# The last attention's tail scores in eight array tiles, and its full products in column tiles

## The chip, the cores and the metric

One core of a Trainium2 chip runs the whole program. The time is the device time of one execution, in microseconds (us). The median of three runs of the kernel before is given, and one further execution was taken with the hardware profiler.

## What is computed

The input `x` holds 16 batches of 256 channels by 512 positions. Four layers follow one another, each added to its input: a masked self-attention with 8 heads, a causal convolution of four taps, a GRU over 128 steps, and a second masked self-attention with 16 heads of 16 channels. Only the last layer is touched by the change:

```python
Q, K, V = (proj(Wq), proj(Wk), proj(Wv))          # 16 heads of 16 channels, 512 positions
att = einsum('bhqd,bhkd->bhqk', Q, K) / sqrt(Dh) + b[0]
att = att * m + (1 - m) * NEG_INF                 # m: 0/1 mask of the keys
y = einsum('bhqk,bhkd->bhqd', softmax(att), V)
x = x + y
```

The masks are drawn with a chance of about one half. Where no batch has more than 320 keys that count, the program takes the way described here. All numbers are fp32.

## The kernel before

The convolution and the recurrence are done together, and at about 1690 us `attend_together` begins the last attention. For each batch it gathers the keys that count into a table of `ROOM` = 320 rows: POOL scatters the rows to a table in memory (`send`), SyncE brings the table back (`fetch_table`). The 320 keys are three chunks, two of 128 and a tail of 64 (`TAILK`).

The 16 heads of a batch are worked in four groups of four heads. A head takes 32 rows (`R3`) of a 128-row tile: 16 rows of its own channels in one half, and one extra row that carries the mask or the maximum. Even and odd heads of a pair of tiles share the projection, made by one product of 128 columns (`heads`, L1381).

A group (`group`) does this:

- *Maxima.* Scores of the queries against the keys, heads in four row tiles of 32 rows (L1415, in two parts), and for the tail in two row tiles of 64 rows against keys laid out on a diagonal (L1421; `diagonal` writes that layout into the last 128 columns of `K`). DVE takes the maxima out of PSUM (L1430, L1435).
- *Shift.* The maxima are transposed (L1448) and added into the extra row of `Q`.
- *Scores for the exponentials.* Keys on the partitions, queries along the columns. For chunks 0 and 1 there are four products, one per head, on row tiles of 32 rows (L1461), each into a PSUM bank of its own. For the tail there are two products on row tiles of 64 rows, each for two heads: partitions 0 to 63 of the result belong to the one head, 64 to 127 to the other. ACT takes the exponentials into `E`, two banks at a time (L1468).
- *Weighing.* Each head's exponentials are multiplied with its values into 32 of the 128 partitions of one bank, so in four column tiles of 32 columns (L1475). For the tail the values `V3` hold an even head on partitions 0 to 63 and an odd one on 64 to 127, and two column tiles of 64 columns do it (L1479). ACT copies the sum out (L1488).

`gather` transposes the batch (L1323, L1338) and makes the values (L1351), which ACT spreads into `V` (L1360, L1366); `finish` divides by the sums of the exponentials and adds the input, on POOL, SyncE and DVE.

PSUM is eight banks: three pairs (`pairs`, tiles `s`) for scores, one bank (`banks`, `sm`) for transposes, projections and values, one (`accs`, `av`) for the weighed sum. A pair is held from the first product into it until its last reader is done.

The order of the instructions is made by a planner (`Plan`) before the program is built. Each piece of work is a node with an engine, an assumed duration, a priority (`gn`, the number of the group, and an offset), its predecessors and the buffers it takes. Repeatedly the planner looks at all nodes that could start, and takes, among those within 0.12 us of the earliest, the one of best priority. For TensorE a node also has a mode, its tiling: a change of mode adds 0.2 us, and a node of the current mode has its priority bettered by 0.25. On the chip the engines run this fixed order, and wait on semaphores.

Of the kernel before, what the change touches and what calls it, by code (L numbers as in the profile page):

```python
# [16 lines left out]
P = 128  # L17
# [233 lines left out]
def tile_kernel(ctx: ExitStack, tc: tile.TileContext, x, cond, Wq0, Wo0, W_ih, W_hh, b_ih, b_hh,  # L251
# [999 lines left out]
    def attend_together():  # L1251
# [3 lines left out]
        with ExitStack() as es:  # L1255
# [8 lines left out]

            NK, G, TAILK = 3, H3 * R3 // P, ROOM - 2 * P
# [3 lines left out]
            V3 = [t[:, 2].rearrange("p (m q s) r -> p m q s r", m=2, q=2) for t in V]  # L1269
# [23 lines left out]
            for i in range(2):  # L1293
                nc.gpsimd.memset(V[i], 0.0)
                for q, e in ((0, DK3), (1, 0)):
                    nc.gpsimd.memset(V[i][:, 0:2, q::2, e : e + 1], 1.0)
                    for odd in range(2):
                        nc.gpsimd.memset(V3[i][64 * odd : 64 * odd + 64, :, q, odd::2, e : e + 1], 1.0)
                nc.gpsimd.memset(NM[i], 0.0)

            def gather(b, g0):
# [42 lines left out]
                for c0 in range(0, NK, 2):  # L1344
# [3 lines left out]
                    def values(some=some, sm=sm, c0=c0):  # L1348
                        for c in some:
                            for kc in range(KC):  # L1350
                                nc.tensor.matmul(SM[sm.i][:, (c - c0) * D : (c - c0 + 1) * D],  # L1351
                                                 lhsT=XK[xk.i][:, kc, c * P : c * P + P], rhs=wv3T[:, kc],
                                                 start=(kc == 0), stop=(kc == KC - 1))
                    m = plan.add("PE", 0.86 * len(some), g0 - 1.6 + 0.2 * c0, moved + v_done + [banks.take(sm)] + ([] if c0 else [vs.take(v)]), values)
                    for c in some:
                        def spread(c=c, sm=sm, c0=c0):
                            src = SM[sm.i][:, (c - c0) * D : (c - c0 + 1) * D]
                            if c < 2:
                                dst = V[v.i][:, c].rearrange("p (h q) r -> p h (q r)", q=2).rearrange("p h (m i) -> p h m i", i=DK3)
                                nc.scalar.copy(dst[:, :, 0::3], src.rearrange("p (h m i) -> p h m i", m=2, i=DK3))  # L1360
                                return
                            src = src.rearrange("p (m s q i) -> p m s q i", m=2, q=2, i=DK3)
                            for q in range(2):
                                for odd in range(2):
                                    r = slice(64 * odd, 64 * odd + 64)
                                    nc.scalar.copy(V3[v.i][r, :, q, odd::2, DK3 * q : DK3 * q + DK3], src[r, :, odd::2, q])  # L1366
                        m2 = plan.add("ACT", 0.4 if c < 2 else 1.0, g0 - 1.6, [m], spread)
# [4 lines left out]
            def heads(b, hp, g0, mk, xk, x3, moved, turned, made):  # L1372
# [3 lines left out]
                for w, x_, X_, deps, name, n, dur in ((wq3T, x3, X3, turned, "q", T, 1.72), (wk3T, xk, XK, moved + [made], "k", ROOM, 1.1)):  # L1376
                    sm = banks.new()

                    def product(w=w, x_=x_, X_=X_, n=n, sm=sm):
                        for kc in range(KC):  # L1380
                            nc.tensor.matmul(SM[sm.i][:, 0:n], lhsT=w[:, kc, hp * P : (hp + 1) * P], rhs=X_[x_.i][:, kc, 0:n],  # L1381
                                             start=(kc == 0), stop=(kc == KC - 1))
                    m = plan.add("PE", dur, gp - 2.6 + 0.1 * (name == "k"), deps + [banks.take(sm)] + [(qs if name == "q" else ks).take(x) for x in (qt if name == "q" else kt)], product)
# [19 lines left out]
            def group(g, b, gn, qt, kt, ready, v, v_done):  # L1403
# [50 lines left out]
                for kc in range(NK):  # L1454
                    e = es_.new()
                    st = [pairs.new() for _ in range(2 if kc < 2 else 1)]

                    def scores(kc=kc, st=st):
                        for j in range(J if kc < 2 else 2):
                            r = slice(R * j, R * j + R) if kc < 2 else slice(2 * R * j, 2 * R * j + 2 * R)  # L1460
                            nc.tensor.matmul(S[st[j // 2].i][:, j % 2, :], lhsT=K[kt.i][r, kc * P : kc * P + P] if kc < 2 else K[kt.i][r, ROOM:],  # L1461
                                             rhs=Q[qt.i][r, :], start=True, stop=True)
                    m = plan.add("PE", 0.88, gn + kc / NK, [shifted] + [pairs.take(x) for x in st], scores, mode=32 if kc < 2 else 64)
                    scored.append(m)
                    done = []
                    for jp in range(len(st)):
                        x = plan.add("ACT", 1.05, gn + kc / NK, [m] + (done or [es_.take(e)]),
                                     lambda jp=jp, st=st, e=e: nc.scalar.activation(E[e.i][:, 2 * jp : 2 * jp + 2], S[st[jp].i], AF.Exp))  # L1468
# [3 lines left out]
                    def weigh(kc=kc, e=e):  # L1472
                        if kc < 2:
                            for j in range(J):
                                nc.tensor.matmul(AV[acc.i][R * j : R * j + R, :], lhsT=V[v.i][:, kc, 8 * (g // 2) + 2 * j + q],  # L1475
                                                 rhs=E[e.i][:, j], start=(kc == 0), stop=False)
                            return
                        for jp in range(2):
                            nc.tensor.matmul(AV[acc.i][2 * R * jp : 2 * R * jp + 2 * R, :],  # L1479
                                             lhsT=V3[v.i][:, g // 2, q, 2 * jp : 2 * jp + 2].rearrange("p s r -> p (s r)"),  # L1480
                                             rhs=E[e.i][:, jp], start=False, stop=True)
                    last = plan.add("PE", 0.88, gn + kc / NK + 0.2, done + v_done + ([accs.take(acc)] if kc == 0 else [last]), weigh,
                                    mode="c32" if kc < 2 else "c64")
# [93 lines left out]
```

## Time and profile before

| what | us |
|---|---|
| median of 3 runs | 2614.56 |
| lowest, highest | 2605.72, 2616.25 |
| the profiled execution: its time | 2617.86 |
| the profiled execution: its span, first to last instruction | 2616.1 |
| TensorE busy, share of the span | 2448.6, 94% |
| VectorE (DVE) busy | 1780.2, 68% |
| ScalarE (ACT) busy | 1016.1, 39% |
| granted TensorE clock, mean | 0.977 |

A line of a group names the kernel's line, the engine and operation, the tiles written and read, the part of the array used (rows*columns), and the size streamed. An fp32 product appears as two records, so four products in four tiles are x8. Records of one tiling overlap, so a record's duration isn't its cost: the distance from one piece's start to the next one's is. In the chain of work, `smC` is the single bank, `sC` the pairs, `avC` the weighed sum.

### The profile page before, as it was taken

The numbers are of one execution on the slowest core, as the hardware profiler recorded it, in microseconds if no ns is written. First come the engines' busy times: TensorE is split into PE (matmuls) and PEld (weight loads), VectorE is DVE, ScalarE is ACT, GpSimd is POOL, SyncE is SP. The second block draws the span as 40 slices with busy tenths as digits, with TensorE's granted clock in tenths as the row PEclk, the third lists the DMA queues.
The fourth block names the chain that finished last, engine by engine and source line by source line (L and its number), as shares of the span: only waits on it lengthen the run. The fifth ranks groups of instructions, "written<-read, shape, count | busy, mean of one in ns | idle before, by whom it ended". The sixth has DMA issues, their size and how long they took to land.

```text
span 2616.1 us, 100684 instructions
## 1 busy us (share of the span) xinstructions
PE 2448.6 (94%) x45506; PEld 1635.2 (63%) x45506; DVE 1780.2 (68%) x3810; ACT 1016.1 (39%) x2459; POOL 385.3 (15%) x382
## 2 busy tenths in 40 slices
PE   5999889959999999999999999789999999999995
PEld 3545444437888888888888888644444444444442
DVE  1578778866888888888888655455666566665652
ACT  2444444422333333333333332234444544555452
POOL 2333231210000000000000000132223222231113
PEclk9999999979999999999999999989999999999997
DMA  5222221130000000000000000010011100110001
GB/s 178 69 65 68 62 63 35 35 137 3 5 4 4 5 4 4 4 5 4 4 4 5 5 4 4 5 49 28 28 32 36 41 29 28 33 39 26 19 19 36
DMA packets 54738, 80.22 MB, mean 31 GB/s; under 512 B 15824, under 2 KB 33434, under 8 KB 54292
## 3 DMA queue, kind: packets, MB, share of 16 engines
q1 hardware_dynamic: 45076, 56.66, 7.1%
q0 software_dynamic: 9216, 16.96, 2.2%
q8 instruction: 360, 5.90, 1.0%
q14 instruction: 86, 0.70, 0.1%
HBM read 45.05 MB, written 36.75 MB: 31 GB/s over the span
## 4 chain that ended last, share of the span: by engine, by line
PE 80%; issue 6%; DMA 4%; DVE 4%; POOL 3%; ACT 1%; SPq 0%; POOLq 0%; another core or an unknown queue 0%; DVEq 0%; ACTq 0%
PE pr L1084 10%; PE pz L1084 9%; PE pn L1084 9%; PE sC L1461 8%; PE sC L1415 7%; PE avC L1475 5%; PE pt L1075 4%; PE pr L1063 4%; PE pz L1063 4%; PE smC L1381 4%; PE sC L1421 3%; PE avC L1479 2%; PE smA L908 2%; DMA backA<-result,goto 2%; PE smC L1351 2%
## 5 line engine op out<-in xcount | busy, mean ns | idle before, releaser
L1430 DVE TENSOR_REDUCE nmC<-sC 128x4 f32<-128x1024 f32 x256 | 301.8, 1221 | 208.5 <-PE sC L1415 206.8
L1468 ACT ACTIVATE wih<-sC 128x1024 f32<-128x1024 f32 x320 | 313.6, 1022 | 236.6 <-PE sC L1461 218.6
L1084 PE MATMUL pr<-whh,hist 128*32 128x128 f32 x8192 | 281.6, 275 | 14.2 <-DVE hist L1120 10.2
L1084 PEld LDWEIGHTS pr<-whh,hist 128*32 128x32 f32 x8192 | 218.8, 110 | 118.5 <-DVE hist L1120 51.1
L1084 PE MATMUL pz<-whh,hist 128*32 128x128 f32 x8192 | 279.6, 273 | 2.2 <-issue 2.2
L1084 PE MATMUL pn<-whh,hist 128*32 128x128 f32 x8192 | 278.9, 273 | 0.0
L533 DVE SCALAR_TENSOR_TENSOR yw<-xT,condT,yw 128x512 f32<-128x512 f32 x360 | 269.5, 749 | 6.8
L1063 PE MATMUL pr<-wih,xw 128*32 128x128 f32 x4096 | 222.6, 274 | 22.2 <-DMA wv3nat<-in_L_cond_Wv_dram 19.1
L1084 PEld LDWEIGHTS pz<-whh,hist 128*32 128x32 f32 x8192 | 237.3, 110 | 3.3 <-issue 3.0
L1084 PEld LDWEIGHTS pn<-whh,hist 128*32 128x32 f32 x8192 | 237.1, 110 | 0.1
L1461 PE MATMUL sC<-qC,kC 32*128 32x512 f32 (+1 forms) x1280 | 231.7, 632 | 0.4 <-ACT wih L1468 0.3
L1063 PE MATMUL pz<-wih,xw 128*32 128x128 f32 x4096 | 224.1, 274 | 3.7 <-issue 3.4
L1115 ACT ACTIVATE nn<-pre 128x64 f32<-128x64 f32 x256 | 65.7, 257 | 384.3 <-DVE pre L1113 377.0
L1108 ACT ACTIVATE r<-pr 128x128 f32<-128x128 f32 x256 | 71.0, 277 | 319.2 <-PE pr L1084 318.9
L881 DVE TENSOR_REDUCE whh<-smA 128x2 f32<-128x640 f32 (+2 forms) x211 | 150.2, 752 | 65.1 <-PE smA L873 46.2
L1415 PE MATMUL sC<-kC,qC 32*128 32x256 f32 x2048 | 185.5, 401 | 0.0
L297 POOL DMA_INDIRECT table<-xT,togo x128 | 133.5, 1043 | 248.2 <-DMA table<-xT,togo 169.4
L1516 POOL TENSOR_TENSOR aC<-aC,pbC 128x512 f32<-128x512 f32 x64 | 81.2, 1270 | 590.9 <-ACT wih L1468 287.7
L1075 PE MATMUL pt<-xw,wih 128*32 128x256 f32 x2048 | 166.8, 382 | 0.0
L1288 POOL MEMSET pbC<- 128x512 f32 x4 | 2.3, 625 | 1101.2 <-DVE xT L1092 1101.2
L1109 DVE STREAM_TRANSPOSE rT<-r 128x128 f32<-128x128 f32 x256 | 79.7, 311 | 118.8 <-ACT r L1108 102.4
L1415 PEld LDWEIGHTS sC<-kC,qC 32*128 32x128 f32 x2048 | 128.7, 184 | 46.2 <-issue 16.5
(178 smaller groups left out, 3853.8 us busy)
## 6 DMA issues: line engine op xcount, KB each, us to landing
xA<-in_x_dram SPq DMA_DIRECT2D x16, 512.0 KB
pbC<-sums SPq DMA_DIRECT2D x256, 32.0 KB
out_dram<-oC SPq DMA_DIRECT2D x32, 256.0 KB
table<-zeros SPq DMA_DIRECT2D x16, 320.0 KB
xsA<-table SPq DMA_DIRECT2D x16, 256.0 KB
result<-ocA SPq DMA_DIRECT2D x16, 256.0 KB
xsC<-table SPq DMA_DIRECT2D x16, 256.0 KB
wih<-in_L_cond_W_ih_dram SPq DMA_DIRECT2D x4, 768.0 KB
```

What stands on the lines that cost most here:

```text
L297: nc.gpsimd.indirect_dma_start(tables[b], bass.IndirectOffsetOnAxis(togo[:, f, b : b + 1], 0), xT[:, f, b], None, bounds_check=ROOM - 1, o ...
L533: nc.vector.scalar_tensor_tensor(acc, xT[:, f, :, lo : lo + WIN], condT[:, f, k : k + 1], xT[:, f, :, t0 : t0 + WIN] if k == 0 else acc, A ...
L881: nc.vector.tensor_reduce(dst[:, lo : lo + len(some)], SM[0:n, some[0] : some[-1] + 1, 0:ROOM], AX.X, ALU.max, negate=True)
L1063: nc.tensor.matmul(sets[k % 2][0 if g == GATE_R else 2][32 * j : 32 * j + 32].rearrange("p (f i) -> p f i", i=32), lhsT=x2, rhs=gates(wih, ...
L1075: nc.tensor.matmul(ps[32 * j : 32 * j + 32], lhsT=wih[:, kc, 2 * T + fo * P + 32 * j : 2 * T + fo * P + 32 * j + 32], rhs=parts[p][:, kc]. ...
L1084: nc.tensor.matmul(ps[32 * j : 32 * j + 32].rearrange("p (f i) -> p f i", i=32), lhsT=slot[:, f], rhs=gates(whh, f, j)[:, g], start=False, ...
L1381: nc.tensor.matmul(SM[sm.i][:, 0:n], lhsT=w[:, kc, hp * P : (hp + 1) * P], rhs=X_[x_.i][:, kc, 0:n], start=(kc == 0), stop=(kc == KC - 1))
L1415: nc.tensor.matmul(S[st[j // 2].i][:, j % 2, u * 2 * P : (u + 1) * 2 * P], lhsT=Q[qt.i][R * j : R * j + R, c : c + P], rhs=K[kt.i][R * j : ...
L1430: nc.vector.tensor_reduce(dst[:, :, :, e_at + 1], S[st[jp].i].rearrange("p j (u k) -> p j u k", u=2), AX.X, ALU.max, negate=True)
L1461: nc.tensor.matmul(S[st[j // 2].i][:, j % 2, :], lhsT=K[kt.i][r, kc * P : kc * P + P] if kc < 2 else K[kt.i][r, ROOM:], rhs=Q[qt.i][r, :], ...
L1468: lambda jp=jp, st=st, e=e: nc.scalar.activation(E[e.i][:, 2 * jp : 2 * jp + 2], S[st[jp].i], AF.Exp))
L1475: nc.tensor.matmul(AV[acc.i][R * j : R * j + R, :], lhsT=V[v.i][:, kc, 8 * (g // 2) + 2 * j + q], rhs=E[e.i][:, j], start=(kc == 0), stop= ...
```

## The change

The tail's scores for the exponentials are made by eight products instead of two: four heads (row tiles of 32 rows) by two halves of the queries (column tiles of 64 columns). A bank then holds one head: its tail keys against queries 0 to 255 on partitions 0 to 63, and against queries 256 to 511 on partitions 64 to 127, in 256 columns. These take two pairs where one was taken. Two exponentials of 2 x 256 columns replace one of 2 x 512.

The tail's values are kept twice, `V` chunk 2 with zeros on partitions 64 to 127 and `V4` with zeros on 0 to 63. The tail is weighed by eight products in four column tiles of 32 columns: for each half of the queries, each head, 256 columns over all 128 partitions, with the zeros dropping the other half.

The projections and the values are made by a new function, `columns`, in four column tiles of 32 columns in place of one product of 128, and get the planner's mode of the weighing, "c32". The tail scores have a mode of their own, "8". The planner's durations for the tail scores, their exponentials and the spreading of the tail's values are changed.

```diff
-            V3 = [t[:, 2].rearrange("p (m q s) r -> p m q s r", m=2, q=2) for t in V]
+            V4 = [work.tile([P, H3, R3], F32, tag=f"v4{i}", name=f"v4C{i}") for i in range(2)]
+            HALF = T // 2
...
                 nc.gpsimd.memset(V[i], 0.0)
+                nc.gpsimd.memset(V4[i], 0.0)
                 for q, e in ((0, DK3), (1, 0)):
                     nc.gpsimd.memset(V[i][:, 0:2, q::2, e : e + 1], 1.0)
-                    for odd in range(2):
-                        nc.gpsimd.memset(V3[i][64 * odd : 64 * odd + 64, :, q, odd::2, e : e + 1], 1.0)
+                    nc.gpsimd.memset(V[i][0:64, 2, q::2, e : e + 1], 1.0)
+                    nc.gpsimd.memset(V4[i][64:P, q::2, e : e + 1], 1.0)
...
+            def columns(ps, left, right, kc):
+
+                for j in range(4):
+                    r = slice(R3 * j, R3 * j + R3)
+                    nc.tensor.matmul(ps[r], lhsT=left[:, r], rhs=right, start=(kc == 0), stop=(kc == KC - 1))
...
-                                nc.tensor.matmul(SM[sm.i][:, (c - c0) * D : (c - c0 + 1) * D],
-                                                 lhsT=XK[xk.i][:, kc, c * P : c * P + P], rhs=wv3T[:, kc],
-                                                 start=(kc == 0), stop=(kc == KC - 1))
-                    m = plan.add("PE", 0.86 * len(some), g0 - 1.6 + 0.2 * c0, moved + v_done + [banks.take(sm)] + ([] if c0 else [vs.take(v)]), values)
+                                columns(SM[sm.i][:, (c - c0) * D : (c - c0 + 1) * D], XK[xk.i][:, kc, c * P : c * P + P], wv3T[:, kc], kc)
+                    m = plan.add("PE", 0.86 * len(some), g0 - 1.6 + 0.2 * c0, moved + v_done + [banks.take(sm)] + ([] if c0 else [vs.take(v)]), values, mode="c32")
...
-                            for q in range(2):
-                                for odd in range(2):
-                                    r = slice(64 * odd, 64 * odd + 64)
-                                    nc.scalar.copy(V3[v.i][r, :, q, odd::2, DK3 * q : DK3 * q + DK3], src[r, :, odd::2, q])
-                        m2 = plan.add("ACT", 0.4 if c < 2 else 1.0, g0 - 1.6, [m], spread)
+                            for dst, r in ((V[v.i][:, c], slice(0, P)),) if c < 2 else ((V[v.i][:, 2], slice(0, 64)), (V4[v.i], slice(64, P))):
+                                dst = dst.rearrange("p (h q) r -> p h (q r)", q=2).rearrange("p h (m i) -> p h m i", i=DK3)
+                                nc.scalar.copy(dst[r, :, 0::3], src[r].rearrange("p (h m i) -> p h m i", m=2, i=DK3))
+                        m2 = plan.add("ACT", 0.4 if c < 2 else 0.7, g0 - 1.6, [m], spread)
...
-                            nc.tensor.matmul(SM[sm.i][:, 0:n], lhsT=w[:, kc, hp * P : (hp + 1) * P], rhs=X_[x_.i][:, kc, 0:n],
-                                             start=(kc == 0), stop=(kc == KC - 1))
-                    m = plan.add("PE", dur, gp - 2.6 + 0.1 * (name == "k"), deps + [banks.take(sm)] + [(qs if name == "q" else ks).take(x) for x in (qt if name == "q" else kt)], product)
+                            columns(SM[sm.i][:, 0:n], w[:, kc, hp * P : (hp + 1) * P], X_[x_.i][:, kc, 0:n], kc)
+                    m = plan.add("PE", dur, gp - 2.6 + 0.1 * (name == "k"), deps + [banks.take(sm)] + [(qs if name == "q" else ks).take(x) for x in (qt if name == "q" else kt)], product, mode="c32")
...
-                    st = [pairs.new() for _ in range(2 if kc < 2 else 1)]
+                    st = [pairs.new() for _ in range(2)]
 
                     def scores(kc=kc, st=st):
-                        for j in range(J if kc < 2 else 2):
-                            r = slice(R * j, R * j + R) if kc < 2 else slice(2 * R * j, 2 * R * j + 2 * R)
-                            nc.tensor.matmul(S[st[j // 2].i][:, j % 2, :], lhsT=K[kt.i][r, kc * P : kc * P + P] if kc < 2 else K[kt.i][r, ROOM:],
-                                             rhs=Q[qt.i][r, :], start=True, stop=True)
-                    m = plan.add("PE", 0.88, gn + kc / NK, [shifted] + [pairs.take(x) for x in st], scores, mode=32 if kc < 2 else 64)
+                        for c in range(1 if kc < 2 else 2):
+                            for j in range(J):
+                                r, bank = slice(R * j, R * j + R), S[st[j // 2].i][:, j % 2]
+                                if kc < 2:
+                                    nc.tensor.matmul(bank, lhsT=K[kt.i][r, kc * P : kc * P + P], rhs=Q[qt.i][r, :], start=True, stop=True)
+                                else:
+                                    nc.tensor.matmul(bank[64 * c : 64 * c + 64, 0:HALF], lhsT=K[kt.i][r, 2 * P : ROOM],
+                                                     rhs=Q[qt.i][r, HALF * c : HALF * (c + 1)], start=True, stop=True)
+                    m = plan.add("PE", 0.88 if kc < 2 else 0.45, gn + kc / NK, [shifted] + [pairs.take(x) for x in st], scores, mode=32 if kc < 2 else "8")
...
-                        x = plan.add("ACT", 1.05, gn + kc / NK, [m] + (done or [es_.take(e)]),
-                                     lambda jp=jp, st=st, e=e: nc.scalar.activation(E[e.i][:, 2 * jp : 2 * jp + 2], S[st[jp].i], AF.Exp))
+                        n = T if kc < 2 else HALF
+                        x = plan.add("ACT", 1.05 if kc < 2 else 0.6, gn + kc / NK, [m] + (done or [es_.take(e)]), lambda jp=jp, st=st, e=e, n=n:
+                                     nc.scalar.activation(E[e.i][:, 2 * jp : 2 * jp + 2, 0:n], S[st[jp].i][:, :, 0:n], AF.Exp))
...
-                        for jp in range(2):
-                            nc.tensor.matmul(AV[acc.i][2 * R * jp : 2 * R * jp + 2 * R, :],
-                                             lhsT=V3[v.i][:, g // 2, q, 2 * jp : 2 * jp + 2].rearrange("p s r -> p (s r)"),
-                                             rhs=E[e.i][:, jp], start=False, stop=True)
-                    last = plan.add("PE", 0.88, gn + kc / NK + 0.2, done + v_done + ([accs.take(acc)] if kc == 0 else [last]), weigh,
-                                    mode="c32" if kc < 2 else "c64")
+                        for h in range(2):
+                            for j in range(J):
+                                head = 8 * (g // 2) + 2 * j + q
+                                nc.tensor.matmul(AV[acc.i][R * j : R * j + R, HALF * h : HALF * (h + 1)],
+                                                 lhsT=V4[v.i][:, head] if h else V[v.i][:, 2, head],
+                                                 rhs=E[e.i][:, j, 0:HALF], start=False, stop=True, skip_group_check=True)
+                    last = plan.add("PE", 0.88, gn + kc / NK + 0.2, done + v_done + ([accs.take(acc)] if kc == 0 else [last]), weigh, mode="c32")
```

More of the change, by code (lines that the diff above doesn't have):

```diff
@@ L1357, in spread @@
                             src = SM[sm.i][:, (c - c0) * D : (c - c0 + 1) * D]
[L1358 to L1362, printed above, removed]
-                            for q in range(2):
-                                for odd in range(2):
-                                    r = slice(64 * odd, 64 * odd + 64)
-                                    nc.scalar.copy(V3[v.i][r, :, q, odd::2, DK3 * q : DK3 * q + DK3], src[r, :, odd::2, q])
-                        m2 = plan.add("ACT", 0.4 if c < 2 else 1.0, g0 - 1.6, [m], spread)
+                            for dst, r in ((V[v.i][:, c], slice(0, P)),) if c < 2 else ((V[v.i][:, 2], slice(0, 64)), (V4[v.i], slice(64, P))):
+                                dst = dst.rearrange("p (h q) r -> p h (q r)", q=2).rearrange("p h (m i) -> p h m i", i=DK3)
+                                nc.scalar.copy(dst[r, :, 0::3], src[r].rearrange("p (h m i) -> p h m i", m=2, i=DK3))
+                        m2 = plan.add("ACT", 0.4 if c < 2 else 0.7, g0 - 1.6, [m], spread)
                         v_done.append(m2)
@@ L1475, in weigh @@
                                 nc.tensor.matmul(AV[acc.i][R * j : R * j + R, :], lhsT=V[v.i][:, kc, 8 * (g // 2) + 2 * j + q],
-                                                 rhs=E[e.i][:, j], start=(kc == 0), stop=False)
+                                                 rhs=E[e.i][:, j], start=(kc == 0), stop=(kc == 1), skip_group_check=True)
                             return
-                        for jp in range(2):
-                            nc.tensor.matmul(AV[acc.i][2 * R * jp : 2 * R * jp + 2 * R, :],
-                                             lhsT=V3[v.i][:, g // 2, q, 2 * jp : 2 * jp + 2].rearrange("p s r -> p (s r)"),
-                                             rhs=E[e.i][:, jp], start=False, stop=True)
-                    last = plan.add("PE", 0.88, gn + kc / NK + 0.2, done + v_done + ([accs.take(acc)] if kc == 0 else [last]), weigh,
-                                    mode="c32" if kc < 2 else "c64")
+                        for h in range(2):
[5 more added lines that the diff above has]
+                    last = plan.add("PE", 0.88, gn + kc / NK + 0.2, done + v_done + ([accs.take(acc)] if kc == 0 else [last]), weigh, mode="c32")
                     es_.free(e, last)
```

## The prediction

> **What bounds the kernel now.** I read the page first, then the busy times of 100 us stretches, then the chain of work over one batch of the last attention, and last the order in time around single pieces.
>
> The page, head and first part, and one stretch of the last attention (busy us of each engine with its instruction count, then granted clock, DMA share, GB/s):
>
> ```profile
> span 2616.1 us, 100684 instructions
> PE 2448.6 (94%) x45506; PEld 1635.2 (63%) x45506; DVE 1780.2 (68%) x3810; ACT 1016.1 (39%) x2459; POOL 385.3 (15%) x382
> ...
> 2000.00:2100.00 100.00, 100.00 (x756) 47.28 (x754) 60.78 (x92) 50.04 (x73) 27.97 (x24) 1.00 0.13 36
> ```
>
> From about 1710 us to 2585 us the last attention runs, and TensorE is never out of work by this count; DVE is at 61%, ACT at 50%, at full clock. A busy TensorE isn't a TensorE at its peak, so the chain matters: pieces in order of time (start, us, what) over one batch of four groups.
>
> ```profile
> 2001.18 1.10 PE sC L1415 x16
> 2002.28 0.99 PE avC L1475 x8
> 2003.28 1.27 PE smC L1381 x4
> 2004.55 1.01 PE avC L1479 x4
> 2005.56 1.07 PE sC L1461 x8
> 2006.63 0.59 PE smC L1448 x4
> 2007.22 1.72 PE sC L1415 x14
> 2008.94 0.99 PE avC L1475 x8
> 2009.93 1.09 PE sC L1421 x16
> 2011.03 0.86 PE sC L1461 x4
> 2011.89 1.92 PE smC L1351 x8
> ...
> 2042.47 1.10 PE sC L1415 x16
> 2043.57 1.06 PE sC L1461 x4
> 2044.62 0.59 PE smC L1338 x4
> 2045.21 1.74 PE sC L1461 x8
> ```
>
> Every piece of the chain is TensorE's, and the period is 54.2 us a batch (the piece of 2001.18 comes again at 2055.34). Two kinds of loss show. First, nearly every piece is of another tiling than its neighbour: x8 of L1475 is two rounds of four 512-column products, and costs 1.00 us. In the recurrence the same tiling (128 rows by 32 columns) flows without a break:
>
> ```profile
> 1002.22 1.12 PE L1084 MATMUL pr<-whh,hist 128*32 128x128 f32 x32
> 1003.10 1.12 PE L1084 MATMUL pn<-whh,hist 128*32 128x128 f32 x32
> ```
>
> The reader is to take start from start: 32 records in 0.875 us, so four 128-column records per 0.109 us, hence 0.87 us for L1475's eight of 512. The other 0.13 us is the change of tiling. Second, waits: L1415 is 1.72 us where 1.10 is its undisturbed time, L1461 1.74 against 1.07. They wait for PSUM pairs: three pairs of banks, each held until DVE's maxima (L1430, 1221 ns for a pair) or ACT's exponentials (L1468, 1022 ns) are done. Summed over the steady part these waits are about 2.7 us a batch.
>
> **What the Trainium skill says.** "TensorEngine Tiling (Array Packing)", Key Properties: changing the tiling mode drains the array, changing only the tile within a mode doesn't. The trace agrees: 1.00 against 0.87 us. Its section Restrictions and Gotchas says that tiles of different rows may not write one PSUM bank at once; so the eight tiles need the four banks of two pairs. "TensorE: Matmul & The Clock Gate", Part 3, reports sixteen tiles of rows and columns running together at 10.6 times one; no run here shows eight, only four tiles of 32 rows by 64 columns:
>
> ```profile
> 293.05 0.77 PE L873 MATMUL smA<-whh 32*64 32x320 f32 x8
> 293.74 0.75 PE L934 MATMUL smA<-wih,whh 128*32 128x320 f32 x8
> ```
>
> From start to start that is 0.69 us for two passes of 320 columns.
>
> **The change part by part**, per batch of four groups.
>
> *Tail scores.* Now four records of 512 columns on two tiles: 0.96 us in three groups (after L1421, same tiling), 1.06 in the fourth. Then sixteen records of 256 columns on eight tiles. If all eight run together, two passes of 256 columns: 0.69 less 2 x 64 columns at 0.109/128 us each = 0.58, and a little for eight more issues: 0.62. If only four run together, 0.43 more: 1.05. I take 0.62, since column tiles and row tiles each overlap fully in the trace. Gain 3 x 0.34 + 0.44 = 1.46. L1421 loses its neighbour of the same tiling in three groups: 0.99 becomes 1.09, +0.30. Net -1.16 (the other end: 3 x 0.09 + 0.30 = +0.57 worse).
>
> *Weighing.* The tail's four records of 512 columns become sixteen of 256 on four column tiles: four rounds of 0.216 against two of 0.43, equal. Its gain is the tiling, which is now that of L1475.
>
> *Full products.* L1381 and L1351 issue 16 records where 4 stood; streaming is equal, since the four column tiles share the time (recurrence rate above). Weight loads of 32 columns (108 ns) replace one of 128 (184-195 ns): the exposed first load shrinks by some 0.05 us a piece. With the order kept, three chains become one tiling: L1475, k product, L1479: 0.99 + 1.27 + 1.01 = 3.27 to 0.87 + 1.07 + 1.00 = 2.94; L1475, L1479: -0.14; L1475, q product, L1479: 3.92 to 3.58. Pieces left alone (one q, one k, two of values): 4 x 0.06. Sum -0.33 - 0.14 - 0.34 - 0.23 = -1.04. The extra issues are free: from 1600 to 1700 us, in the recurrence, TensorE issues 51 instructions a us, loads counted; this stage issues 15 and would issue some 22 (360 more a batch).
>
> *Exponentials.* One of 1024 elements (1022 ns) becomes two of 512; the nearest row is the copy out of PSUM of that shape, L1488, 584 ns. +0.15 us a group on ACT, covered by its idle half; uncovered it would be 0.6 us a batch. Spreading the tail's values: four copies of 206 ns become two at about 375 ns (L1360), -0.07.
>
> *Pairs.* The new wait. The tail's scores take two pairs instead of one. The code runs over the column half outside and heads inside, so if the second pair is late, the first pair's other half stands behind that wait on TensorE's queue, and no exponential begins. I placed the new pieces by hand among the measured ends of DVE and ACT, order kept. Second group (2007 us): both pairs are free at 2010.7, the values' products cover the rest: no extra wait. Third (2020): the next scores wait for the tail maxima's pair, 0.24 extra. First (2047): the second pair of maxima is free only at 2051.1, 0.54. Fourth (2042): maxima, tail scores and scores follow each other, the first pair is free at 2044.9: 0.75. Together 1.5 us. The planner can put projections into these holes; with perfect cover it is 0, and with later pieces made late in turn up to 3. I take 0.9.
>
> *POOL at the start.* Two memsets of 128x512 (610 ns each) ahead of the first scatter; TensorE waits 5.08 us for that chain at 1707 us. +1.2 us once.
>
> Sum: (-1.16 - 1.04 + 0.9) x 16 batches = -20.8, +1.2: -19.6 us. The profiled execution took 2617.86 us (span 2616.1), so 2598; against the median of the runs shown, 2614.56, the same step gives **2595 us**. The end (2585 us on: sums, reciprocal, output, 31 us of DMA and POOL) is untouched.
>
> **The rivals.** (1) *Pairs take it all, and more.* The extra wait is 0.9 in my sum; at 2.2 us a batch the change is worth nothing, beyond 3.0 it is slower by over 0.5%. For it: by the rows' durations pairs are held some 30 us per group of 3 x 13.5 now, 31 of 3 x 13.2 then, and every group already waits for one. Against: the tail's pairs come free soon (0.6 us exponentials). At 3.7: +25 us, 2640. (2) *The order stays as it is and all 1.5 us of wait is paid*: -0.7 x 16 + 1.2 = -10, 2605: no measurable change. The same would come of eight tiles running four by four: +1.73 on the scores with little pair trouble, 2608. (3) *The planner uses the new tiling well*: values' products set beside the weighing too (another 3 x 0.13), pairs covered: -2.6 x 16 + 1.2 = -40, 2574.
>
> **How the numbers follow.** 0.5% is 13 us, about what a measurement of this kernel can tell from no change. My case 0.42 (2595, own range 2585 to 2606, a small part of it within 0.5%), rival 3 0.18, rival 2 0.19, rival 1 0.21. Faster 0.57, same 0.22, slower 0.21. The range reaches from rival 3's better end, 2570, to 2632, short of rival 1's full size.
>
> **What would show it.** Right: tail scores at 0.6 to 0.7 us from start to start; L1475 at 0.87 us before another piece of its tiling; a period of 52.9 us a batch. Wrong: tail scores above 1 us; more pieces of L1415 and L1461 over 1.5 us than now, or TensorE idle before them for ACT's exponentials; first scores later than 1720 us by more than 2 us. The likeliest error is the planner's new order, which I can't read off the trace of before: it places all 51 pieces of a batch anew.

## The result, and the profile after

The kernel with the change takes 2622.44 us (median; 2614.21 to 2631.14) beside 2609.93 us (2605.72 to 2621.83) of the kernel before, measured together. The ratio is 1.0035, with a 95% interval of 1.0022 to 1.0049: slower by 0.35%, some 9 us (the medians alone are 12.5 us apart). The forecast was 2595, and faster.

The page of the kernel after, its head, its first part and the shares of the chain of work, and below these the same shares of the kernel before:

```profile
span 2617.1 us, 106544 instructions
PE 2438.6 (93%) x48386; PEld 1622.6 (62%) x48386; DVE 1777.8 (68%) x3810; ACT 1019.6 (39%) x2491; POOL 386.1 (15%) x384
...
PE 74%; DVE 9%; issue 8%; DMA 5%; POOL 3%; ACT 1%; SPq 0%; POOLq 0%; DVEq 0%; ACTq 0%
...
PE 80%; issue 6%; DMA 4%; DVE 4%; POOL 3%; ACT 1%; SPq 0%; POOLq 0%; another core or an unknown queue 0%; DVEq 0%; ACTq 0%
```

One execution was profiled of each, and their spans are nearly equal (2616.1 and 2617.1 us) because the recurrence, which the change leaves alone, ended 5.1 us earlier in this one. From the end of its last product (L1084) to the end of the program it is 933.3 us before and 939.4 after. The shares tell more: in the kernel before TensorE held 80% of the chain and DVE 4%; now it is 74% and 9%. The same stretch of the last attention as before (busy us of each engine, clock, DMA share, GB/s):

```profile
2000.00:2100.00 100.00, 99.36 (x1085) 46.52 (x1078) 59.62 (x92) 51.26 (x78) 28.06 (x24) 1.00 0.12 37
```

TensorE is "busy" for 99.36 of 100 us here too, so this count can't show what was won or lost. The new groups (from 1780 to 2500 us, by shape; busy us and mean ns of one record) show that the new pieces do what they should:

```profile
L1475 ACT ACTIVATE wih<-sC 128x512 f32<-128x512 f32 x106 | 57.5, 594 | 88.3 <-PE sC L1467 81.2 <-ACT v4C L1369 3.6 <-DVE nmC L1444 3.5
L1467 PE MATMUL sC<-qC,kC 32*64 32x256 f32 x848 | 41.6, 400 | 0.0
```

The exponential of 512 elements takes 594 ns (584 in the forecast). A record's 400 ns isn't the cost of a tail score: from start to start its 16 records take 0.62 us, as the chain shows. Here is that chain over the worst stretch of a batch (start, us, what):

```profile
2034.66 1.08 PE smC L1310 x16
2035.74 0.62 PE sC L1467 x16
...
2037.94 1.23 PE sC L1417 x16
...
2039.26 1.04 issue
2040.30 0.90 DVE nmC L1432
2041.20 0.23 issue
2041.44 1.28 DVE ntC L1437 x2
2042.71 2.27 DVE nmC L1432 x2
```

The tail's scores (L1467) flow at 0.62 us. But from 2039 to 2045 us the chain runs over DVE's maxima (L1432, L1437). It does so again from 2047 to 2050. The chain of the kernel before had no such piece in a whole batch. Two pieces in order of time point to the reason (start, us, what, and in brackets the idle time before it with what ended it):

```profile
2035.90 1.01 DVE L1391 SCALAR_TENSOR_TENSOR kC<-smC,C,mkC 128x320 f32<-128x320 f32 x2 [7.38 <-ACT wih L1475]
...
2043.90 0.30 PEld L1465 LDWEIGHTS sC<-qC,kC 32*128 32x128 f32 x4 [0.83 <-DVE nmC L1432]
```

DVE had stood idle for 7.38 us when it came to lay out the next keys. The profile puts that down to an exponential, but the keys' product (the L1310 of 2034.66, 1.08 us), which this instruction reads, had only just ended: the order has it no earlier. From 2038 to 2052 us the maxima of two groups and two sets of chunk scores then all ask for pairs, and the second half of a set of scores (the weight loads of 2043.90) waits for maxima to let go of a pair.

**Work and waits.** I took each TensorE piece's distance from its start to the next one's, and subtracted its undisturbed time (maxima 1.09, chunk scores 1.07, tail scores 0.96 before and 0.62 after); what is over is called a wait. A piece that is shorter than that, as the tail's maxima are beside a piece of their own tiling, isn't set against it (with it the 3.0 below would be the 2.7 of the prediction). The period is that of the copies of the weighed sum over batches 2 to 13; waits are from 1860 to 2460 us.

| kernel | period, us/batch | waits | the rest: work |
|---|---|---|---|
| before | 54.18 | 3.0 (maxima 1.9, chunk scores 1.0, tail scores 0.1) | 51.2 |
| after | 54.64 | 5.3 (maxima 1.7, chunk scores 3.1, tail scores 0.5) | 49.3 |

The change takes 1.9 us of work out of a batch and puts 2.3 us of waiting in. The periods differ by 0.46 us; in 16 batches this is 7.4 us, and the trace shows 6.1 from the end of the recurrence on. Score and maxima pieces of over 1.5 us are 44 in these 600 us before and 65 after. Maxima pieces stay nearly the same (32 and 33); those of the chunk scores (L1461, then L1465) go from 12 to 32, and from 1.72 to 2.03 us each. Three of a batch's eight are long. One follows the tail's scores directly, and its second half waits for the tail's exponentials; the other two wait for maxima to let go of a pair.

These 6 to 7 us are the traced execution's. Part of what was measured may come from TensorE's granted clock. It is 0.977 in both profiled executions, but 0.970 to 0.977 in the 11 of the kernel after: four at 0.975 or above took 2618 us on average, seven at 0.972 or below 2625. The kernel before had medians of 0.975 to 0.977 in the four measurements for the experiments; for the one here its clocks aren't on record. So how much of the 9 us is clock stays open.

### The profile page after: what moved, and what is told of

Same layout as the page of the kernel before. It is cut to its first block, busy times and chain, and to the rows that moved or that the text cites. A ratio compares the mean times of both kernels' runs of the same rounds, so it can differ in the third digit from the quotient of the medians.

```text
span 2617.1 us, 106544 instructions
## 1 busy us (share of the span) xinstructions
PE 2438.6 (93%) x48386; PEld 1622.6 (62%) x48386; DVE 1777.8 (68%) x3810; ACT 1019.6 (39%) x2491; POOL 386.1 (15%) x384
## 4 chain that ended last, share of the span: by engine, by line
PE 74%; DVE 9%; issue 8%; DMA 5%; POOL 3%; ACT 1%; SPq 0%; POOLq 0%; DVEq 0%; ACTq 0%
PE pr L1084 10%; PE pz L1084 9%; PE pn L1084 9%; PE sC L1417 5%; PE smC L1310 5%; PE sC L1465 5%; PE pt L1075 4%; PE pr L1063 4%; PE avC L1482 4%; PE pz L1063 4%; DVE nmC L1432 3%; PE smA L908 2%; PE avC L1488 2%; DMA backA<-result,goto 2%; DVE ntC L1437 2%
## 5 line engine op out<-in xcount | busy, mean ns | idle before, releaser
L1475 ACT ACTIVATE wih<-sC 128x1024 f32<-128x1024 f32 (+1 forms) x384 | 320.1, 881 | 264.2 <-PE sC L1465 148.6
L1432 DVE TENSOR_REDUCE nmC<-sC 128x4 f32<-128x1024 f32 x256 | 301.5, 1219 | 71.2 <-PE sC L1417 70.8
L1084 PE MATMUL pr<-whh,hist 128*32 128x128 f32 x8192 | 281.2, 275 | 13.8 <-DVE hist L1120 9.8
L1084 PEld LDWEIGHTS pr<-whh,hist 128*32 128x32 f32 x8192 | 218.3, 110 | 117.9 <-DVE hist L1120 50.4
L1084 PE MATMUL pz<-whh,hist 128*32 128x128 f32 x8192 | 279.4, 273 | 3.3 <-issue 3.1
L1084 PE MATMUL pn<-whh,hist 128*32 128x128 f32 x8192 | 278.3, 273 | 0.0
L1084 PEld LDWEIGHTS pz<-whh,hist 128*32 128x32 f32 x8192 | 236.4, 110 | 4.9 <-issue 4.9
L1084 PEld LDWEIGHTS pn<-whh,hist 128*32 128x32 f32 x8192 | 236.5, 110 | 0.2
L1465 PE MATMUL sC<-qC,kC 32*128 32x512 f32 x1024 | 186.3, 643 | 2.9 <-DVE nmC L1432 2.5
L1417 PE MATMUL sC<-kC,qC 32*128 32x256 f32 x2048 | 173.5, 402 | 1.9 <-DVE nmC L1432 0.6
L1391 DVE SCALAR_TENSOR_TENSOR kC<-smC,C,mkC 128x320 f32<-128x320 f32 x64 | 32.4, 546 | 187.0 <-PE smC L1310 100.6
```

The source lines that it names most:

```text
L1084: nc.tensor.matmul(ps[32 * j : 32 * j + 32].rearrange("p (f i) -> p f i", i=32), lhsT=slot[:, f], rhs=gates(whh, f, j)[:, g], start=False, ...
L1417: nc.tensor.matmul(S[st[j // 2].i][:, j % 2, u * 2 * P : (u + 1) * 2 * P], lhsT=Q[qt.i][R * j : R * j + R, c : c + P], rhs=K[kt.i][R * j : ...
L1432: nc.vector.tensor_reduce(dst[:, :, :, e_at + 1], S[st[jp].i].rearrange("p j (u k) -> p j u k", u=2), AX.X, ALU.max, negate=True)
L1465: nc.tensor.matmul(bank, lhsT=K[kt.i][r, kc * P : kc * P + P], rhs=Q[qt.i][r, :], start=True, stop=True)
L1475: nc.scalar.activation(E[e.i][:, 2 * jp : 2 * jp + 2, 0:n], S[st[jp].i][:, :, 0:n], AF.Exp))
```

## The experiments

Two theories stood against each other. **P**, the pairs: the tail's scores now hold two of the three pairs, and this makes the waits. **O**, the order: the planner, given other durations and tilings, happens on a worse order, and a good one would keep the gain. All ratios are to the kernel before, measured together on the same chip; its median moved between 2608 and 2621 us from one chip to another, so that ratios are to be compared, and not times from different chips. To tell whether two kernels have the same order, I compared the sequence of their pieces by kind over eleven batches.

**The parts alone.** Only the full products in column tiles:

```diff
+            def columns(ps, left, right, kc): ...
-                                nc.tensor.matmul(SM[sm.i][:, ...], lhsT=XK[...], rhs=wv3T[:, kc], ...)
+                                columns(SM[sm.i][:, ...], XK[...], wv3T[:, kc], kc)
-                            nc.tensor.matmul(SM[sm.i][:, 0:n], lhsT=w[...], rhs=X_[x_.i][:, kc, 0:n], ...)
+                            columns(SM[sm.i][:, 0:n], w[...], X_[x_.i][:, kc, 0:n], kc)
```

and mode "c32" for both. What was expected:

> Only the full products go into column tiles (with the planner's mode of the weighing); the tail stays as before. Theory P (the tail's second PSUM pair takes back more than its faster scores give): the products' own gain stays, less than in the full change because the tail's weighing keeps its tiling of 64 columns: two joints of one tiling and the smaller change of tiling, some 0.6 us a batch, about 10 us faster than before (2600). Theory C (the column-tiled products themselves cost the time, by more instructions or by a worse order): slower than before by 5 us or more.

Measured: 0.9971 (0.9962 to 0.9981), 2606.12 us; period 53.64, waits 3.1. Work falls by 0.7 us a batch and waits rise by 0.1. This part alone is a gain, of 0.29%, about what was expected. TensorE's order is that of before, piece for piece, in spite of the new mode.

Only the tail: the kernel after with the two calls of `columns` back to whole products and no mode. The eight tiles, the second pair and the zero-padded values stay:

> Only the tail part: eight tiles, two pairs, zero-padded values, weighing in four column tiles; the full products stay whole. Theory P: slower than the full change, by what the products gave, so 2630 us or more, with the tail scores still at 0.62 us. Theory C: at or below the time of before, 2590 to 2610 us.

Measured: 1.0156 (1.0135 to 1.0178), 2654.40 us; period 56.47, waits 6.2. Work falls by 0.9 us, where 1.16 was forecast, and waits rise by 3.2. Some of both is the clock: within these batches it was granted at half twice, for 6.8 us each, which by an estimate from these lengths is up to 0.6 us a batch. The two parts don't add: -0.54 and +2.29 us of period make +1.75, and together they cost +0.46. The tail alone got an order of its own: only some four tenths of its pieces stand in the sequence of the kernel before, and about as many in that of the kernel after.

**The second pair without the gain.** In the kernel before, the tail's two products go to two pairs, one bank of each, with two exponentials of 512 elements; TensorE's work is the same:

```diff
-                    st = [pairs.new() for _ in range(2 if kc < 2 else 1)]
+                    st = [pairs.new() for _ in range(2)]
...
-                            nc.tensor.matmul(S[st[j // 2].i][:, j % 2, :], ...
+                            nc.tensor.matmul(S[st[j // 2 if kc < 2 else j].i][:, j % 2 if kc < 2 else 0, :], ...
...
+                        w = 2 if kc < 2 else 1
-                                     ... nc.scalar.activation(E[e.i][:, 2 * jp : 2 * jp + 2], S[st[jp].i], AF.Exp))
+                                     ... nc.scalar.activation(E[e.i][:, w * jp : w * jp + w], S[st[jp].i][:, 0:w], AF.Exp))
```

(the planner's duration of such an exponential is 0.6, as in the kernel after.)

> The kernel before, but the two banks of the tail's scores lie in two pairs, one bank of each, and ACT takes each with an exponential of its own of 512 elements. TensorE's work is that of before. Theory P: the second pair alone costs what the full change lost and more, since here nothing is won: 2.2 us a batch or more, 2645 us or above. Rival O (the loss is the order that the planner came to in the full change, not the second pair): within 10 us of before.

Measured: 1.0081 (1.0057 to 1.0105), 2636.22 us; period 55.69, waits 4.3, so work is 51.4, nearly unchanged. Slower, but by about two thirds of what was expected. Its chain (start, us, what) has the kernel after's pattern:

```profile
2029.40 1.11 PE sC L1421 x16
2030.54 1.29 DVE ntC L1435 x2
2031.83 0.43 DVE whh L1340
```

After L1421, TensorE's next piece in the chain comes at 2035.90: DVE's maxima and a copy stand between; the copy (L1340) frees the single bank for the next product. The order, though, is not that of before: some nine tenths of TensorE's pieces stand in the sequence of the kernel after, and four tenths in that of before. So the 1.3 us of waits a batch are the price of the second pair together with the order that the planner made for it, and this run doesn't tell P from O.

**The change in the order of before.** The planner got before's modes and durations and one pair for the tail's scores; the second was chosen, as the order was written out, among pairs that were read out by then, and a piece that found none was put back:

```diff
-                    m = plan.add("PE", 0.88 if kc < 2 else 0.45, gn + kc / NK, ..., mode=32 if kc < 2 else "8")
+                    m = plan.add("PE", 0.88, gn + kc / NK, ..., mode=32 if kc < 2 else 64)
+                    m.pairs, m.more = st, kc == 2
...
+                        if kc == 2:
+                            both.append(min((i for i in range(3) if i != both[0]), key=lambda i: (reads[i], used.index(i))))
```

> The changed kernel's instructions, planned with the durations, modes and the single tail pair of the kernel before, so that its order is that of before; a node is put back only where its second pair isn't yet read out. Theory O (the loss is the new order): the prediction's hand placement holds, 1.5 us of added waits a batch against 2.2 won, so 2598 to 2604 us. Theory P (the second pair itself, in any order): the added waits are 2.2 us a batch or more, 2610 us or above.

Measured: 1.0110 (1.0086 to 1.0133), 2643.22 us; period 55.87. The order is before's: over eleven batches TensorE's, DVE's and ACT's pieces stand in exactly its sequence. Work is 49.1 us a batch, as in the kernel after, and waits are 6.8: 3.8 more than before, where O expected 1.5 and P 2.2 or more. (Half clock, 3.4 us twice in these batches, is at most 0.3 of it.) So this run decides against O: the tail's new form with its second pair costs more than the change wins in the order of before too, and the planner's new order took 1.2 us off this loss instead of causing it.

Of the 3.8 us, maxima have 0.8, the tail's own scores 1.4 and chunk scores 1.6. At the chunk scores TensorE now stands idle three times a batch before they start, 2.2 us together, while waits within them fell by 0.6. One of the three (start, us, what, and in brackets the idle time with what ended it):

```profile
2005.43 0.69 PE L1480 MATMUL sC<-qC,kC 32*64 32x256 f32 x16
2006.05 0.66 PE L1349 MATMUL smC<-C,xT 128*128 128x128 f32 x4
2006.27 1.08 ACT L1490 ACTIVATE wih<-sC 128x512 f32<-128x512 f32 x2 [3.13 <-PE sC L1480]
2007.40 1.14 PE L1478 MATMUL sC<-qC,kC 32*128 32x512 f32 x8 [0.70 <-ACT wih L1490]
```

The tail's scores (L1480) hold two of the three pairs until both exponentials (L1490) are done, at 2007.35. The next chunk scores (L1478) want two pairs, and only one short transpose lies between. At the same place in the kernel before, where the tail held one pair, they lost 0.18 us (L1461 at 2052.17 in its chain, 1.25 us against 1.07).

**Less time in the pairs.** DVE takes the maxima over the first half of the keys only, so part of the computation is left out, and a pair of maxima comes free sooner. The same edit on the kernel before and on the kernel after:

```diff
-                                nc.vector.tensor_reduce(dst[:, :, :, e_at + 1], S[st[jp].i].rearrange("p j (u k) -> p j u k", u=2),
+                                nc.vector.tensor_reduce(dst[:, :, :, e_at + 1], S[st[jp].i].rearrange("p j (u k) -> p j u k", u=2)[:, :, :, 0:P],
...
-                                src = S[st[0].i][:, pair].rearrange("p (c j k) -> p c j k", c=NT, j=2)
+                                src = S[st[0].i][:, pair].rearrange("p (c j k) -> p c j k", c=NT, j=2)[:, :, :, 0:32]
```

> The kernel before in its order, but DVE takes each maximum over half of the keys only, so that its reductions take some 0.7 us a pair instead of 1.22 and pairs come free sooner. It is the measure for the same cut in the changed kernel. Both theories: most of the waits on the maxima (1.9 of 3.0 us a batch, before L1415) go, so 2575 to 2595 us.

> The changed kernel in its order with the same cut: maxima over half of the keys only. Theory P (too few free pairs; DVE holds them): the waits fall from 5.4 us a batch to under 3, and the work saved on TensorE shows: 15 to 32 us faster than the kernel before with the same cut, so some 2560. Theory O (the new order is bad whatever the pairs cost): it stays 5 us or more behind the kernel before with the same cut.

Measured: before with maxima over half of the keys 0.9977 (0.9967 to 0.9986), period 54.00, waits 2.8. After with maxima over half of the keys 0.9914 (0.9886 to 0.9943), period 53.08, waits 3.8. On the kernel before I missed: it gives 6 us, not 20 or more. The view of waits has, for that kernel with all keys (us in total, times, longest):

```profile
PEld sC L1415 <- ACT wih L1468: 10.8, 15, 0.8
PEld sC L1415 <- DVE nmC L1430: 10.5, 13, 0.8
```

Half of what its maxima products wait for, by this view, is an exponential to leave a pair; a faster DVE doesn't help there. On the kernel after it takes 1.5 us a batch off the waits, all of it from the chunk scores, and the ranking of the two kernels turns: after is then 0.63% (0.9914 against 0.9977, some 17 us) faster than before. The order of each is as it was. So the changed kernel's waits are waits for pairs, and its saved work is a gain as soon as pairs come free sooner. That is what P says; but O would allow it too, since a bad order also shows as waits for pairs. It is the run in before's order that tells them apart.

**The order alone.** The planner's own constants were sought anew, for the kernel before and for the kernel after each apart. The instructions stay the same, only their order differs:

```diff
 before, order                                     after, order
-            plan, LEADS = Plan(), 1.8             -            plan, LEADS = Plan(), 1.8
+            plan, LEADS = Plan(), 1.9             +            plan, LEADS = Plan(), 1.6
+            plan.STAY = 0.1                       +            plan.STAY = 0
+            plan.SLACK, plan.HOP = 0.3, 0.1       +            plan.SLACK, plan.HOP = 0.3, 0.1
 transposes of a batch: g0 - 3.6 -> g0 - 3.2       transposes of a batch: g0 - 3.6 -> g0 - 4
 products: gp - 2.6 + 0.1 * (name == "k")          products: the same as left
        -> gp - 2.2 + 0.3 * (name == "k")          tail's maxima: gn - LEADS + 2 / 3 -> gn - LEADS + 1
 weighing: + 0.2 -> + 0.4                          tail's scores: gn + 2 / 3 -> gn + 0.4; weighing: + 0.4
```

(`STAY` is the bonus for the current mode, `SLACK` the span within which priority decides, `HOP` the time added where a piece follows one of another engine.)

> The kernel before with other planner constants alone (margin 0.3 us instead of 0.12, hop 0.1 instead of 0.15, stay 0.1 instead of 0.25, weighing 0.2 later in priority, queries' and keys' products 0.4 and 0.2 later, maxima's lead 1.9). No instruction changes, only the order. Theory O (order decides, and the change was measured in a poor one): the waits fall from 3.0 to about 1 us a batch, 2580 us or below. Theory P (three pairs bound it in any order): within 10 us of before.

> The changed kernel with planner constants sought for it in the same way (margin 0.3, hop 0.1, stay 0, weighing 0.2 later, tail scores 0.27 earlier, tail maxima 0.33 later, maxima's lead 1.6). Theory O: the change keeps its 2 us a batch in a good order, so it ends 20 to 30 us below the kernel before in its own good order, under 2560. Theory P: the second pair costs in any order; no faster than the kernel before in its good order, 2580 to 2590.

Measured: before in its new order 0.9867 (0.9844 to 0.9890), 2586.32 us, waits 0.56; after in its new order 0.9874 (0.9849 to 0.9898), 2587.34 us, waits 2.4. Both beat both kernels, by some 35 us, four times what the change costs. But between them there is no difference, and O, which put the changed kernel 20 to 30 us below, fails here too, as far as constants were sought: that no better order exists for the changed kernel isn't shown. In periods: 52.05 less 0.56 leaves 51.5 us of work, 52.11 less 2.4 leaves 49.7. The change takes out 1.8 us of work and puts in 1.8 us of waits. The chain of before in its new order (start, us, what) shows what a stretch without waits looks like:

```profile
2013.13 1.09 PE sC L1425 x16
2014.22 1.92 PE smC L1355 x8
2016.15 1.07 PE sC L1465 x8
2017.22 1.91 PE smC L1385 x4
2019.13 1.10 PE sC L1419 x16
```

Every piece that takes pairs (L1419, L1425, L1465) is followed by one that takes none, and all run in their undisturbed time. In 600 us one score or maxima piece is over 1.5 us long, where 44 were. In the changed kernel's new order 35 are, all of them chunk scores: 11 single sets, and 12 pairs of sets back to back.

The part that gained alone, the column tiles, with constants of its own (`SLACK` 0.2, `HOP` 0.1, `STAY` 0.35, products from gp - 2.2, tail's maxima + 0.8, weighing + 0.4):

> Full products in column tiles, tail as before, with planner constants sought for it (margin 0.2, hop 0.1, stay 0.35, weighing 0.2 later, queries' products 0.4 later, tail maxima 0.13 later). If the products' gain of 0.5 us a batch stands beside the good order's 2.1, some 43 us below the kernel before, 8 us below the kernel before in its good order. If the good order already hides the changes of tiling, no better than that one, 34 us below the kernel before.

Measured: 0.9879 (0.9859 to 0.9899), 2582.34 us; period 52.16, waits 1.25. Not to be told from before's own new order: 0.6 us of work were won against it, and 0.7 us of waits came in.

**The smallest change of order.** The kernel before, with nothing but a tie decided otherwise:

```diff
-                    m = plan.add("PE", 0.9, gn - LEADS + part / 3, ready + ...
+                    m = plan.add("PE", 0.9, gn - LEADS + (part / 3 if part < 2 else 0.666667), ready + ...
```

> The kernel before, the tail maxima's priority raised by a third of a millionth, so that ties between two nodes fall the other way. No instruction changes. Theory O in its strong form (the planner's order is chance at the level of the change's 9 us): 5 to 12 us away from before. If the order is stable: no difference.

Measured: 1.0022 (1.0012 to 1.0032); waits 3.5, of which chunk scores 1.6 where they were 1.0. A third of a millionth in one priority costs some 6 us, more than half of what the change costs. So for the size of the loss the strong form of O, that it is within what an order does by chance, can't be excluded. This is one tie only; it doesn't give the spread.

**A faster DVE in the good orders.** The two new orders with the maxima over half of the keys, as above. (The 3.7 us in the second expectation count the second of two sets of scores back to back as a wait; it is 2.4.)

> The kernel before in its good order, maxima over half of the keys only. Its trace has 0.6 us of waits a batch left, so there is little to win: within 10 us of it uncut, some 2580 us.

> The changed kernel in its good order with the same cut. Theory P: its 3.7 us of waits a batch, nearly all of them scores that wait for pairs held by the maxima, fall to 1.5 or less, and the work saved shows: 20 to 35 us below the kernel before in its good order with the same cut, some 2550. If the waits have another cause: equal to it within 8 us.

Measured: 0.9841 (0.9824 to 0.9857) and 0.9817 (0.9795 to 0.9839); 2568.78 and 2563.85 us; waits 0.4 and 1.9. I expected 20 to 35 us between them and found 0.24%, some 6, with intervals that overlap. Here the faster DVE takes only 0.5 us off the changed kernel's waits. The traces show why. Once a batch the changed kernel's new order has two sets of chunk scores (L1469) back to back, which want four pairs of the three there are. First without the faster DVE, then with it:

```profile
2029.94 2.36 DVE L1436 TENSOR_REDUCE nmC<-sC 128x4 f32<-128x1024 f32 x2 [0.16 <-PE sC L1421]
2031.22 0.30 PEld L1469 LDWEIGHTS sC<-qC,kC 32*128 32x128 f32 x4 [1.08 <-DVE nmC L1436]
2032.35 0.31 PEld L1469 LDWEIGHTS sC<-qC,kC 32*128 32x128 f32 x8 [0.83 <-DVE nmC L1436]
...
2022.77 0.30 PEld L1469 LDWEIGHTS sC<-qC,kC 32*128 32x128 f32 x4 [0.30 <-DVE nmC L1436]
2023.37 0.30 PEld L1469 LDWEIGHTS sC<-qC,kC 32*128 32x128 f32 x4 [0.30 <-ACT wih L1479]
```

The first set's second half and then the second set each wait for one of two maxima (L1436): the two sets take 3.56 to 3.61 us, where 2.14 is undisturbed. With the faster DVE they take 3.25 to 3.28, because now the last half waits for an exponential (L1479) of the first set. One more set a batch takes 1.58 us in both kernels and waits for an exponential. So of 2.4 us of waits, 1.4 are held by maxima; but behind the maxima stand the exponentials, so a faster DVE alone doesn't take them away.

## Why the prediction was wrong

Rival 1 came true, just past its break-even: waits rose by 2.3 us a batch where 2.2 was named as the point at which the change is worth nothing. By the prediction's steps:

- *Tail scores: right.* 0.62 us from start to start in the chain, the number taken. Sixteen records of 256 columns, two a product, make eight products on eight tiles. Their cost fits the two passes of 256 columns that the forecast took from the 320-column rows, with all eight tiles running together, and not the 1.05 us of four by four. L1423, which lost its neighbour, is 1.09, as said.
- *Weighing and full products: right in kind, a little too large.* From start to start L1482 takes 0.88 us before a piece of its own tiling and 1.00 else; the tail's weighing is 0.43 to 0.46 and 0.55, 0.99 in all. The q product is 1.74 where it was 1.91, the k product 1.19 to 1.21 where it was 1.27. Together they gave -0.8 us a batch where -1.04 was forecast: the planner set three pieces a batch before one of their own tiling, and the forecast, with before's order kept, counted five. The tail's scores and maxima gave -1.05 of -1.16. Of -2.2 us a batch for both steps, -1.9 came.
- *Exponentials: right.* 594 ns. ACT is busy for 51.26 of 100 us.
- *POOL at the start: too large.* From the first of its memsets to the first scatter it is 8.84 us where it was 8.44: +0.4 us, not +1.2.
- *Pairs: this step failed.* "I take 0.9", out of 1.5 us from placing the new pieces by hand in before's order, with some holes filled by the planner. The trace has 2.3. Two assumptions were wrong. First, the 1.5 us: with before's order kept, the waits rose by 3.8. On the chunk scores that come right after the tail's and want two pairs, while the tail's exponentials still hold two, the placing by hand put 0.24 us, at one place and for the tail maxima's pair; TensorE's idle time before them is 2.2 us. "The tail's pairs come free soon" doesn't hold against a tail score that itself has become short. Second, that the planner would cover the holes down to 0.9. It did lessen the loss, but takes the piece of best priority among those that could start soon, by assumed durations, and made stretches like that from 2036 to 2052 us, where the keys' product comes late and the maxima of two groups and two sets of scores want pairs together. So the wait also sits elsewhere than placed: of +2.3 us, chunk scores have +2.1, the tail's own scores +0.4 and the maxima -0.1.
- *The likeliest error was named* ("the planner's new order"), and it was not the error: the order of before is worse for the changed kernel. But a planner's order did deserve a range of its own: orders of one and the same set of instructions differed by 35 us here. The chance of rival 1, 0.21, was too low for that.

What is shown: in the same order, the sequence of before, the tail's new form with its second pair brings in more waiting (3.8 us a batch) than the change saves in work (2.1), while the full products' new form brings in 0.1; and with pairs freed sooner in the order of the kernel after, the changed kernel is faster than before. What is argued: that the stretch of 2036 to 2052 us is bad because the keys' product is late; no run moved that piece alone. Nor does any run have the second pair by itself in before's order, without the tail's faster scores and its two shorter exponentials. What stays open: how much of the 0.35% a tie could have decided, how much the clock, and whether some order exists in which the change wins.

## What to carry to other kernels

When a faster form of a piece holds more of a shared buffer, price the buffer first: here 1.9 us of TensorE work a batch was won and 2.3 us of waiting for PSUM pairs came in. Look above all at the next piece that wants the buffer: a piece made shorter brings it sooner. When an order comes from a planner, an edit to durations, modes or buffers can draw a new order, so compare the two sequences, run the new instructions in the old order, and measure the plan's own spread (a tie decided otherwise, constants sought anew for both kernels) before a difference of 0.3% is put down to the edit. And where the bound engine is "busy" all the time, measure from start to start.

## What the runs showed of the hardware that was not expected

- Changing only the tie-break of the order, with the same instructions, moved the time by 0.22% (0.12 to 0.32); changing the planner's constants, by 1.33% (1.10 to 1.56).
- Waits of TensorE's weight loads, as the view of waits sums them, aren't time lost. In before's new order the largest such line of the chunk scores is longer than in the kernel after (22.5 against 18.7 us from 1780 to 2500 us), and yet TensorE loses 0.56 us a batch there and 5.3 here. So most of such a wait, up to 0.8 us at a time, lies behind products that still stream:

```profile
PEld sC L1465 <- DVE nmC L1434: 22.5, 38, 0.8
```

- "TensorEngine Tiling (Array Packing)" of the Trainium skill says in Restrictions and Gotchas that tiles of different rows may not write one bank at once. This is why eight tiles took two pairs. No run here tried it otherwise; what the runs show is what the form that obeys it costs, 3.8 us of waits a batch in before's order.
- The granted clock can fall in the midst of steady work. In the run of the tail alone it was at half from 2276 us on for 6.8 us (a stretch of it: us, busy time of each engine, then the clock, here 0.50), and again at 2392 and 2508:

```profile
2277.00:2283.00 6.00, 5.79 (x38) 2.52 (x36) 0.55 (x3) 3.17 (x5) 0.00 (x0) 0.50 0.01 3
```

  Half of a tail's weighing then took 0.86 us from start to start, where it takes 0.46. Each of the first two falls came as TensorE had paused for 0.32 and then 0.48 or 0.49 us; but one batch before the second, at 2335, the same two pauses brought no fall. What decides it no run shows. The kernel before had the full clock in this stretch.
